# Layer 1's factors go through DRAM as rows, GpSimd weights and joins the sums, and one turn follows

## Chip, core and metric

The kernel runs on one core of a Trainium2 chip. All data are float32. The metric is the time of the device in microseconds (us), as the median of several runs. A profile of one execution shows where the time goes. The engines are named as in the profile: PE (TensorE, matmuls), PEld (its weight loads), DVE (VectorE), ACT (ScalarE), POOL (GpSimd) and SP, which issues most DMA transfers.

## The reference

Two layers of attention over a picture of 64 x 64 positions (N = 4096 tokens), with C = 256 channels and a batch of 2. Layer 0 has 4 heads of 16 channels, a normalization, and a factor per row (`dyn`). The change is in layer 1, which has 4 heads of 64 channels:

```
qkv = einsum('oc,bchw->bohw', w_qkv, x) + b_qkv
q, k, v = split(qkv.reshape(b, 4, 192, N), 3, axis=2)
attn = softmax(einsum('bhdn,bhdm->bhnm', q, k) / 8, axis=-1)
out = einsum('bhnm,bhdm->bhnd', attn, v).reshape(b, c, h, w)
return einsum('oc,bchw->bohw', w_out, out) + b_out + x
```

The product of `attn` and `v` is reshaped as it lies (tokens first, then channels) into the shape of the picture. So the kernel needs it with tokens on the partitions before it writes it away.

## The kernel before

Layer 0 is done in blocks of 512 tokens. Behind it, layer 1 goes over 32 units. A unit (b, g, j) is one batch, one pair of heads (g, heads k = 0 and 1) and one block of 512 queries. It has 32 chunks (m) of 128 keys. One pass of the last loop, a step, handles two chunks, so a unit has `US` = 16 steps. The program keeps an order written out by hand: `seq` holds every compute instruction at its place on its engine, and `at(t, place, ...)` hangs an extra piece of work on step t, at the place "start", "early", "early end", "late", "late end" or "end". DMA transfers are issued by SP in the order in which a scheduler places them, and SP waits at each one for what it needs.

For a chunk, PE computes the scores of both heads into PSUM (`score`, L885). DVE folds them into a running maximum (`keep`, L902), and ACT copies them to SBUF (L903). Eleven steps later (`LAG`) DVE adds the negative maximum (`shift`, L960), ACT takes the exponential (`weigh`, L972), POOL adds the weights to a running sum (L982 for the first two chunks, L984 for the others), and PE multiplies with the values (`gather`, L1013). The chunks wait in a ring of 26 buffers (`raw`); a buffer is filled again when POOL and PE have used it.

The maximum is taken in two groups n of 16 chunks. After each group, PE turns the maxima (`turn_max`, L915), DVE reduces them (`fold`, L932), SP writes them to DRAM (`neg`) and reads them back as a row for all partitions (`row`), and ACT places them in PSUM (`place_shift`, L952). The two groups of a unit thus have sums and products of different maxima: `lose` (L945) takes the difference, and `keep_total`, `add_sums` and `factors` make from it and the sums the two factors per query and head, f, in the form of tokens on partitions (POOL L1126, L1127, L1134, DVE L1133). Then `turn_sums` has PE turn each group's product (L1060, into the bank `misc`), `rows` has DVE multiply it with its factor out of PSUM (L1144), and POOL adds the value bias (L1150) and joins the two (L1153). SP writes the result to `att` (L1158).

PSUM has one bank named `misc`. The turns share it with the projections that are made for later units: for the first 24 units keys and values of the next pair of heads (`next_keys`, `next_values`, quarter by quarter, and the ACT copies `k1s` and `v1s`), for the last 8 units the outputs of batch 0 (`project_out`, the ACT copy `y`, and POOL's add L1181). With t1 = t0 + 24 for a unit that starts at step t0, the sums are at t1 + 4 to 8, and the two turns at t1 + 9. A pool `xb` with three buffers holds blocks of x that are fetched for keys, values and queries, in the passage between the layers too (values v0 to v7 of the first unit). The last unit has a path of its own (`last_rows`, `late_sums`), and after it PE finishes batch 1's outputs from `att` (L1295).

Of the kernel before, what the change touches and what calls it, by code (L numbers as in the profile page):

```python
# [8 lines left out]
F32 = mybir.dt.float32  # L9
AF = mybir.ActivationFunctionType  # L10
ALU = mybir.AluOpType
# [3 lines left out]
P = 128  # L15
NB = 512
# [4 lines left out]
D1 = 64  # L21
# [5 lines left out]
def conv_attention_kernel(  # L27
# [19 lines left out]
    nc = tc.nc  # L47
    B, _, N = x.shape
    NJ = N // NB
    NM = N // P  # L50
    PB = NB // P

    const = ctx.enter_context(tc.tile_pool(name="const", bufs=1))
    dram = ctx.enter_context(tc.tile_pool(name="dram", bufs=1, space=bass.MemoryType.DRAM))
# [157 lines left out]
    def at(t, place, step):  # L212
        extras.setdefault((t, place), []).append(step)
# [19 lines left out]
    with own0:  # L233
# [417 lines left out]
        def misc(name):  # L651
            return small_bank[0](name)

        def fetch(key, src, tag="xb", bufs=3, pool=l1x):
            t = pool.tile([P, CC, NB], F32, tag=tag, bufs=bufs, name=f"{tag}_{key}")
            nc.sync.dma_start(out=t, in_=src.rearrange("(c p) n -> p c n", p=P))
            loaded[key] = t
# [110 lines left out]
    with (  # L768
# [6 lines left out]
    ):  # L775
        small_bank[0] = lambda name: psm.tile([P, NB], F32, tag="misc", name=name)
        rmax, negs, rows_in, shifts, raws, accs = {}, {}, {}, {}, {}, {}
        avs1, srows, losts, joined, halves = {}, {}, {}, {}, {}
        rts = [None, None]
        outs = {}  # L780
        halves_of = {}
# [12 lines left out]
        }  # L794
        sum1 = {
            u: dram.tile([NG * 2, NB], F32, tag="sum_{}_{}_{}".format(*u), name=f"sum_{u}")
            for u in units
        }
        first, begun, late = {}, set(), {}
# [120 lines left out]
        def fold(u, n, k):  # L920


            b, g, j = u
            if k == 0:
                negs[u, n] = small.tile(
                    [P, 2, PB], F32, tag="negs", bufs=2 * NG, name=f"negs_{b}_{g}_{j}_{n}"
                )
                rows_in[u, n] = l1.tile(
                    [P, 2, NB], F32, tag="row", bufs=1, name=f"row_{b}_{g}_{j}_{n}"
                )  # L930
            nm, to = negs[u, n][:, k, :], neg1[u, n][k : k + 1, :]
            seq(nc.vector.tensor_reduce(  # L932
                nm, rts[k].rearrange("p (i m) -> p i m", m=P), AX.X, ALU.max, negate=True
            ))
            nc.sync.dma_start(
                out=to.rearrange("o (a p i) -> p (o a) i", p=P, i=2),
                in_=nm.rearrange("p (a i) -> p a i", i=2),
            )
            nc.sync.dma_start(out=rows_in[u, n][:, k, :], in_=to.partition_broadcast(P))

        def lose(u):

# [62 lines left out]
        def gather(t):  # L1005
            u = b, g, j = units[t // NM]
            m = t % NM
            n = m // GS
            if m % GS == 0:
                avs1[u, n] = psv.tile([P, NB], F32, tag="av", name=f"av1_{b}_{g}_{j}_{n}")  # L1010
            v = vs[b, g, m // PB]
            for k in range(2):
                seq(nc.tensor.matmul(  # L1013
                    avs1[u, n][k * D1 : (k + 1) * D1, :], v[:, m % PB, k, :], raws[t][:, k, :],
                    start=(m % GS == 0), stop=(m % GS == GS - 1),
                ))
            if on_tensor(t) and t % 2 == 1 and t != 2 * END - 1:
                late_sums((t - 1, t) if on_tensor(t - 1) else (None, t))
            elif t == 2 * END - 2:
                late_sums((t, t + 1))  # L1020
            raws.pop(t - 2, None)
            if m % GS == GS - 1:
                a = l1.tile([P, NB], F32, tag="avs", name=f"avs1_{b}_{g}_{j}_{n}")
                seq(nc.scalar.copy(a, avs1.pop((u, n))))
                avs1[u, n] = a

# [30 lines left out]
        def turned(a, name):  # L1057
            ps = misc(name)
            for i in range(PB):
                seq(nc.tensor.transpose(ps[:, bass.ts(i, P)], a[:, bass.ts(i, P)], ident))  # L1060
            return ps.rearrange("p (i k d) -> p k i d", k=2, d=D1)
# [67 lines left out]
        def factors(u):  # L1129

            b, g, j = u
            f = small.tile([P, NG, 2, PB], F32, tag="f1", name=f"f1_{b}_{g}_{j}")
            seq(nc.vector.reciprocal(f[:, 1], srows.pop(u)[:, 1]))  # L1133
            seq(nc.gpsimd.tensor_tensor(f[:, 0], f[:, 1], losts.pop(u), ALU.mult))  # L1134
            joined[u] = f

        def turn_sums(u, n):
            avs1[u, n] = turned(avs1[u, n], "turned_{}_{}_{}_{}".format(*u, n))

        def rows(u, n):  # L1140
            b, g, j = u
            ps = avs1.pop((u, n))
            r = l1.tile([P, 2, PB, D1], F32, tag="rows", name=f"rows_{b}_{g}_{j}_{n}")
            seq(nc.vector.tensor_tensor(  # L1144
                r, ps, joined[u][:, n].unsqueeze(3).to_broadcast([P, 2, PB, D1]), ALU.mult
            ))
            if n == 1:
                halves[u] = r
                bias = b1v[:, 2 * g : 2 * g + 2, :].unsqueeze(2).to_broadcast([P, 2, PB, D1])
                seq(nc.gpsimd.tensor_tensor(r, r, bias, ALU.add))  # L1150
                return
            joined.pop(u)
            seq(nc.gpsimd.tensor_tensor(r, r, halves.pop(u), ALU.add))  # L1153


            to = att[b].rearrange("(h q) (s d) -> h (q s) d", h=H, d=D1)
            for k in range(2):
                nc.sync.dma_start(  # L1158
                    out=to[2 * g + k, bass.ts(j, NB), :].rearrange("(i q) d -> q i d", q=P),
                    in_=r[:, k, :, :],  # L1160
                )
# [37 lines left out]
        for n, u in enumerate(units):  # L1199
# [29 lines left out]
            if u != units[-1]:  # L1229
                at(t1 + 4, "late", lambda u=u: total(u))  # L1230
                at(t1 + 5, "start", lambda u=u: keep_total(u))
                at(t1 + 1, "late", lambda u=u: lose(u))
                at(t1 + 7, "late end", lambda u=u: add_sums(u))
                at(t1 + 8, "end", lambda u=u: factors(u))
                for place, k in (("early", 1), ("late", 0)):
                    at(t1 + 9, place, lambda u=u, k=k: turn_sums(u, k))
                    at(t1 + 9, f"{place} end", lambda u=u, k=k: rows(u, k))
            else:
                at(END + 1, "late", lambda u=u: last_lost(u))
                at(END + 4, "early", lambda u=u: late_sums((None, None)))  # L1240
                at(END + 4, "early end", lambda u=u: keep_late(0))
                at(END + 5, "early", lambda u=u: turn_late(0))
                at(END + 5, "early end", lambda u=u: add_late(u, 0))
                at(END + 6, "early", lambda u=u: turn_sums(u, 0))
                at(END + 6, "early end", lambda u=u: first_rows(u))
                at(END + LAG, "late", lambda u=u: turn_late(1))
                at(END + LAG, "late", lambda u=u: add_late(u, 1))
                at(END + LAG, "late", lambda u=u: turn_sums(u, 1))
                at(END + LAG, "late", lambda u=u: last_rows(u))
# [17 lines left out]
        def fetch_last(i, pool, tag, bufs=1):  # L1267

            t = pool.tile([P, CC, NB], F32, tag=tag, bufs=bufs, name=f"x_last_{i}")
            nc.sync.dma_start(out=t, in_=x1[B - 1][i].rearrange("(c p) n -> p c n", p=P))  # L1270
            last_x[i] = t
# [7 lines left out]
        def fetch_second_half(i):  # L1279

            t = ring.tile([P, 2, NB], F32, tag="raw", name=f"att_last_{i}")
            for k in range(2):
                r, n = k * D1, D1 - NB // D1
                nc.sync.dma_start(
                    out=t[r : r + n, :, :].rearrange("p i n -> p (i n)"),
                    in_=att[B - 1][P + r : P + r + n, bass.ts(i, 2 * NB)],
                )
            last_att[i] = t
# [31 lines left out]
            last_half(j, c, ps)  # L1320
            add_half(j, ps, c == 0)

        for i in range(3):
            at(END - 11 + 2 * i, "start", lambda i=i: fetch_last(i, l1x, "xb", 3))
        at(END - 5, "start", lambda: fetch_last(3, l1, "xo"))
        at(END - 3, "start", lambda: fetch_last(4, l1, "ao"))
        at(END - 10, "start", lambda: fetch_first_half(2, l1x, "q", 2))
        for i in range(2):
            at(END - 2, "start", lambda i=i: fetch_first_half(i, l1, "kv", 2))
        for i in range(NJ // 2):  # L1330
            at(END + 3 + i // 2, "start", lambda i=i: fetch_second_half(i))
        for i in range(EARLY, NJ):
            at(END + 5, "start", lambda i=i: fetch_first_half(i, l1o, f"k{i}"))
        for i in range(5, NJ):
            at(END + 5 + (i - 5) // 2, "start", lambda i=i: fetch_last(i, ring, "raw", None))
        FILL = {(END, "early end"): 0, (END + 1, "early"): 1, (END + 2, "early"): 2}
        for (t, place), j in FILL.items():
            at(t, place, lambda j=j: whole_half(j, 0))
# [93 lines left out]
```

## Time and profile before

| | |
|---|---|
| median of 3 runs | 4652.29 us (4652.22 to 4654.23) |
| profiled execution | 4653.08 us, span 4651.2 us |
| granted TensorE clock | 0.997 of full speed |
| PE busy | 4461.5 us, 96% |
| DVE busy | 3894.5 us, 84% |
| ACT busy | 3439.9 us, 74% |
| POOL busy | 2515.1 us, 54% |
| layer 1, from the first score to the last unit's last turn | about 2058 to 4623 us |

The shares are means over two layers: in layer 0 POOL does almost nothing, and in layer 1 it is busy nine tenths of the time. So the profile is read by stages. A line of a group gives the source line, the engine, the operation, output and input by their names with their shapes, the count, and then the busy time, the mean duration in ns, and the idle time of the engine before it with what ended it. A line of the waits gives who waited for whom, with the sum in us, the number of times and the longest. A line of the order in time begins with its start from the span's start and its duration, both in us. Busy PE is modelled and not PE at its peak.

### The profile page before, as it was taken

The numbers are of one execution on the slowest core, as the hardware profiler recorded it, in microseconds if no ns is written. First come the engines' busy times: TensorE is split into PE (matmuls) and PEld (weight loads), VectorE is DVE, ScalarE is ACT, GpSimd is POOL, SyncE is SP. The second block draws the span as 40 slices with busy tenths as digits, with TensorE's granted clock in tenths as the row PEclk, the third lists the DMA queues.
The fourth block names the chain that finished last, engine by engine and source line by source line (L and its number), as shares of the span: only waits on it lengthen the run. The fifth ranks groups of instructions, "written<-read, shape, count | busy, mean of one in ns | idle before, by whom it ended". The sixth has DMA issues, their size and how long they took to land. (4 is left out here: it accounts for less than half of the span.)

```text
span 4651.2 us, 72702 instructions
## 1 busy us (share of the span) xinstructions
PE 4461.5 (96%) x28242; PEld 1497.3 (32%) x28242; DVE 3894.5 (84%) x4506; ACT 3439.9 (74%) x4588; POOL 2515.1 (54%) x1306
## 2 busy tenths in 40 slices
PE   8999999999999999999999999999999999999998
PEld 3433333333333333332333333333333333222222
DVE  6777777777777777539999999999999999999997
ACT  3366666666666666668888888888888888888885
POOL 5300000000000000008999999999999999999995
PEclk9999999999999999999999999999999999999999
DMA  3100000000000000121111221111211112121213
GB/s 100 39 4 20 20 20 15 15 15 15 15 15 15 15 14 14 35 71 41 33 42 35 62 50 37 37 39 42 71 42 37 37 35 62 48 53 37 53 39 111
DMA packets 199689, 174.81 MB, mean 38 GB/s; under 512 B 121256, under 2 KB 122088, under 8 KB 199344
## 3 DMA queue, kind: packets, MB, share of 16 engines
q1 hardware_dynamic: 197488, 169.58, 14.6%
q8 instruction: 221, 3.62, 0.3%
q14 instruction: 124, 1.02, 0.1%
q10 hardware_dynamic: 1856, 0.59, 0.1%
HBM read 127.65 MB, written 42.48 MB: 37 GB/s over the span
## 5 line engine op out<-in xcount | busy, mean ns | idle before, releaser
L984 POOL TENSOR_TENSOR acc<-acc,raw 128x1024 f32<-128x1024 f32 x883 | 2096.0, 2374 | 72.0 <-ACT raw L972 15.1
L402 DVE TENSOR_REDUCE mx<-a 128x1 f32<-128x512 f32 x2048 | 1315.3, 686 | 449.0 <-PE a L398 448.0
L439 ACT ACTIVATE p<-s 128x512 f32<-128x512 f32 x2048 | 1107.9, 595 | 702.1 <-PE a L398 369.4
L885 PE MATMUL s<-q,k 64*128 64x512 f32 x4096 | 1130.4, 637 | 127.6 <-ACT raw L903 121.0
L960 DVE TENSOR_TENSOR raw<-raw,shift 128x1024 f32<-128x1024 f32 x1024 | 1236.8, 1212 | 7.1 <-ACT shift L952 6.2
L436 PE MATMUL s<-q,kT 32*128 32x512 f32 x4096 | 1217.8, 640 | 0.0
L902 DVE TENSOR_TENSOR rmax<-s,rmax 128x1024 f32<-128x1024 f32 x960 | 1169.5, 1218 | 48.3 <-PE s L885 37.3
L972 ACT ACTIVATE raw<-raw 128x1024 f32<-128x1024 f32 x1024 | 1086.1, 1061 | 144.6 <-DVE raw L960 109.2
L903 ACT COPY raw<-s 128x1024 f32<-128x1024 f32 x1024 | 1035.7, 1011 | 166.5 <-DVE rmax L902 105.5
L398 PE MATMUL a<-kT,q 32*128 32x512 f32 x4096 | 1129.2, 643 | 1.4 <-DVE mx L402 1.3
L1013 PE MATMUL av<-raw,v 128*64 128x512 f32 x4096 | 1014.2, 608 | 10.0 <-ACT raw L972 6.5
L451 PE MATMUL av<-p,v 128*32 128x256 f32 (+1 forms) x7904 | 650.1, 399 | 0.6 <-ACT avs L465 0.6
L501 POOL TENSOR_TENSOR f<-f,dyn 128x16 f32<-128x16 f32 x15 | 3.3, 221 | 1027.4 <-DVE f L500 1027.4
L885 PEld LDWEIGHTS s<-q,k 64*128 64x128 f32 x4096 | 316.8, 185 | 704.1 <-ACT raw L903 541.9
L436 PEld LDWEIGHTS s<-q,kT 32*128 32x128 f32 x4096 | 397.0, 183 | 425.9 <-issue 392.8
L1013 PEld LDWEIGHTS av<-raw,v 128*64 128x64 f32 x4096 | 239.7, 135 | 666.5 <-issue 444.6
L451 PEld LDWEIGHTS av<-p,v 128*32 128x32 f32 x7904 | 157.7, 108 | 751.4 <-issue 737.2
L552 POOL TENSOR_SCALAR res<-res 128x1024 f32<-128x1024 f32 x16 | 16.7, 1044 | 659.1 <-ACT res L551 659.1
L398 PEld LDWEIGHTS a<-kT,q 32*128 32x128 f32 x4096 | 305.1, 183 | 31.5 <-DVE mx L402 18.2
L982 POOL TENSOR_TENSOR acc<-raw,raw 128x1024 f32<-128x1024 f32 x64 | 152.7, 2386 | 118.7 <-ACT raw L972 74.8
L932 DVE TENSOR_REDUCE negs<-rt 128x4 f32<-128x512 f32 x126 | 87.0, 690 | 58.5 <-PE rt L915 58.5
L915 PE MATMUL rt<-ident,rmax 128*128 128x128 f32 x504 | 82.7, 287 | 9.3 <-ACT v1s L841 5.7
(335 smaller groups left out, 1767.1 us busy)
## 6 DMA issues: line engine op xcount, KB each, us to landing
row<-neg SPq DMA_DIRECT2D x128, 256.0 KB
x<-in_x_dram SPq DMA_DIRECT2D x16, 512.0 KB
res<-in_x_dram SPq DMA_DIRECT2D x16, 512.0 KB
x<-res SPq DMA_DIRECT2D x16, 512.0 KB
att<-rows SPq DMA_DIRECT2D x62, 128.0 KB
kd<-k1s SPq DMA_DIRECT2D x24, 256.0 KB
vd<-v1s SPq DMA_DIRECT2D x24, 256.0 KB
k<-kd SPq DMA_DIRECT2D x24, 256.0 KB
```

Source lines behind the costliest of these rows:

```text
L398: seq(nc.tensor.matmul(ps, qs0[u][r, bass.ts(i, P)], kTs[b][r, bass.ts(m, NB)], start=True, stop=True,))
L402: seq(nc.vector.tensor_reduce(mxs[u][:, i * H + h, m : m + 1], ps, AX.X, ALU.max))
L436: seq(nc.tensor.matmul(ps, kTs[b][r, bass.ts(m, P)], qs0[u][r, :], start=True, stop=True))
L439: seq(nc.scalar.activation(pt[:, k, :], ps, AF.Exp, scale=D0**-0.5))
L451: seq(nc.tensor.matmul(avs[u][32 * h : 32 * h + 32, cols], vs0[b][:, m, 32 * h : 32 * h + 32], pts[t, h // 2][:, h % 2, cols], start=(m == ...
L885: seq(nc.tensor.matmul(ps[:, k, :], ks[b, g, m // PB][r, bass.ts(m % PB, P)], qs1[u][r, :], start=True, stop=True,))
L902: seq(nc.vector.tensor_tensor(rmax[u, n], ps, before, ALU.max))
L903: seq(nc.scalar.copy(raw, ps))
L960: seq(nc.vector.tensor_tensor(raws[t], raws[t], shifts[u, t % NM // GS], ALU.add))
L972: seq(nc.scalar.activation(p, p, AF.Exp, scale=D1**-0.5))
L984: seq(nc.gpsimd.tensor_tensor(accs[u, n], accs[u, n], p, ALU.add))
L1013: seq(nc.tensor.matmul(avs1[u, n][k * D1 : (k + 1) * D1, :], v[:, m % PB, k, :], raws[t][:, k, :], start=(m % GS == 0), stop=(m % GS == GS ...
```

## The change

The factors f are written to a new DRAM buffer `fac` and read back as rows: `facs`, 512 queries along a row, each head's row repeated over the 64 partitions of its channels. This is the form in which the products lie before they are turned. POOL multiplies each group's product with its row (`weight`, at t1 + 11), adds the two and adds the bias as a value per partition (`join`, at t1 + 12). One turn follows at t1 + 14 (`turn_rows`), and ACT copies it from PSUM to SBUF (`rows`). The two DVE multiplications are gone.

The maxima of both heads are read back with one transfer of 1024 numbers per partition, after the second head's have been written. `xb` has two buffers instead of three, `avs` three instead of two. Near the end, fetches of x for the last outputs move to other buffers and steps, and `att`'s second half is read four steps later.

```diff
-        def fetch(key, src, tag="xb", bufs=3, pool=l1x):
+        def fetch(key, src, tag="xb", bufs=2, pool=l1x):
...
+        fac1 = {
+            u: dram.tile([NG * 2, NB], F32, tag="fac_{}_{}_{}".format(*u), name=f"fac_{u}")
+            for u in units
+        }
...
-            nc.sync.dma_start(out=rows_in[u, n][:, k, :], in_=to.partition_broadcast(P))
+            if k == 1:
+                nc.sync.dma_start(
+                    out=rows_in[u, n].rearrange("p k n -> p (k n)"),
+                    in_=neg1[u, n].rearrange("k n -> (k n)").partition_broadcast(P),
+                )
...
-                a = l1.tile([P, NB], F32, tag="avs", name=f"avs1_{b}_{g}_{j}_{n}")
+                a = l1.tile([P, NB], F32, tag="avs", bufs=3, name=f"avs1_{b}_{g}_{j}_{n}")
...
-            joined[u] = f
+            nc.sync.dma_start(
+                out=fac1[u].rearrange("m (a p i) -> p (m a) i", p=P, i=2),
+                in_=f.rearrange("p n k (a i) -> p (n k a) i", i=2),
+            )
+            joined[u] = []
+            for n in range(NG):
+
+                pool, tag = (l1o, f"k{2 + 5 * n}") if u == units[-2] else (l1, "kv")
+                row = pool.tile([P, NB], F32, tag=tag, name=f"facs_{b}_{g}_{j}_{n}")
+                for k in range(2):
+                    m = 2 * n + k
+                    nc.sync.dma_start(
+                        out=row[k * D1 : (k + 1) * D1, :],
+                        in_=fac1[u][m : m + 1, :].partition_broadcast(D1),
+                    )
+                joined[u].append(row)
+
+        def weight(u, n):
+
+            a = avs1[u, n].rearrange("p (a i m) -> p a i m", m=P, i=2)
+            f = joined[u][n].rearrange("p (a m i) -> p a i m", m=P, i=2)
+            seq(nc.gpsimd.tensor_tensor(a, a, f, ALU.mult))
+
+        def join(u):
+
+            joined.pop(u)
+            a = avs1.pop((u, 0))
+            seq(nc.gpsimd.tensor_tensor(a, a, avs1.pop((u, 1)), ALU.add))
+            seq(nc.gpsimd.tensor_scalar(a, a, b1[:, u[1], 2:3], None, ALU.add))
+            avs1[u] = a
+
+        def turn_rows(u):
+            avs1[u] = turned(avs1[u], "turned_{}_{}_{}".format(*u))
...
-        def rows(u, n):
+        def rows(u):
             b, g, j = u
...
-            seq(nc.vector.tensor_tensor(
-                r, ps, joined[u][:, n].unsqueeze(3).to_broadcast([P, 2, PB, D1]), ALU.mult
-            ))
...
+            r = l1.tile([P, 2, PB, D1], F32, tag="rows", name=f"rows_{b}_{g}_{j}")
+            seq(nc.scalar.copy(r, avs1.pop(u)))
...
-                for place, k in (("early", 1), ("late", 0)):
-                    at(t1 + 9, place, lambda u=u, k=k: turn_sums(u, k))
-                    at(t1 + 9, f"{place} end", lambda u=u, k=k: rows(u, k))
+                for k in range(NG):
+                    at(t1 + 11, ("early end", "late end")[k], lambda u=u, k=k: weight(u, k))
+                at(t1 + 12, "early end", lambda u=u: join(u))
+                at(t1 + 14, "early", lambda u=u: turn_rows(u))
+                at(t1 + 14, "early end", lambda u=u: rows(u))
...
-        for i in range(3):
-            at(END - 11 + 2 * i, "start", lambda i=i: fetch_last(i, l1x, "xb", 3))
-        at(END - 5, "start", lambda: fetch_last(3, l1, "xo"))
-        at(END - 3, "start", lambda: fetch_last(4, l1, "ao"))
+        for i in range(2):
+            at(END - 5 + 3 * i, "start", lambda i=i: fetch_last(i, l1x, "xb", 2))
+        at(END - 4, "start", lambda: fetch_last(2, l1, "xo"))
+        at(END - 3, "start", lambda: fetch_last(3, l1, "ao"))
...
-            at(END + 3 + i // 2, "start", lambda i=i: fetch_second_half(i))
+            at(END + 7 + i // 2, "start", lambda i=i: fetch_second_half(i))
...
-        for i in range(5, NJ):
-            at(END + 5 + (i - 5) // 2, "start", lambda i=i: fetch_last(i, ring, "raw", None))
+        for i in range(4, NJ):
+            at(END + 5 + (i - 4) // 2, "start", lambda i=i: fetch_last(i, ring, "raw", None))
```

More of the change, by code (lines that the diff above doesn't have):

```diff
@@ L777, in conv_attention_kernel @@
         rmax, negs, rows_in, shifts, raws, accs = {}, {}, {}, {}, {}, {}
-        avs1, srows, losts, joined, halves = {}, {}, {}, {}, {}
+        avs1, srows, losts, joined = {}, {}, {}, {}
         rts = [None, None]
@@ L1137, in turn_sums @@
         def turn_sums(u, n):
             avs1[u, n] = turned(avs1[u, n], "turned_{}_{}_{}_{}".format(*u, n))
-        def rows(u, n):
+        def rows(u):
             b, g, j = u
-            ps = avs1.pop((u, n))
-            r = l1.tile([P, 2, PB, D1], F32, tag="rows", name=f"rows_{b}_{g}_{j}_{n}")
-            seq(nc.vector.tensor_tensor(
-                r, ps, joined[u][:, n].unsqueeze(3).to_broadcast([P, 2, PB, D1]), ALU.mult
-            ))
[L1147 to L1153, printed above, removed]
+            r = l1.tile([P, 2, PB, D1], F32, tag="rows", name=f"rows_{b}_{g}_{j}")
+            seq(nc.scalar.copy(r, avs1.pop(u)))
```

## The prediction

> **What bounds the kernel now.** I read the groups of layer 1 first, then the waits of VectorE and of GpSimd within single units, then the order in time. The groups from 2150 us on (columns: busy us, mean ns, idle before and who ended it):
>
> ```profile
> L984 POOL TENSOR_TENSOR acc<-acc,raw 128x1024 f32<-128x1024 f32 x868 | 2060.4, 2374 | 69.5 <-ACT raw L972 13.7
> L960 DVE TENSOR_TENSOR raw<-raw,shift 128x1024 f32<-128x1024 f32 x1003 | 1211.5, 1212 | 5.0 <-ACT shift L952 4.1
> ...
> L1144 DVE TENSOR_TENSOR rows<-turned,f 128x512 f32<-128x512 f32 x62 | 42.4, 683 | 1.2 <-issue 1.2
> ...
> L1153 POOL TENSOR_TENSOR rows<-rows,rows 128x512 f32<-128x512 f32 x31 | 39.8, 1282 | 2.3
> L1150 POOL TENSOR_TENSOR rows<-rows,b1v 128x512 f32<-128x512 f32 x31 | 39.7, 1280 | 0.0
> ```
>
> The view of stretches shows four engines near their limit: of 2300 to 2600 us, PE is busy 283.1, DVE 287.0, ACT 265.8, POOL 280.3. So I take one unit (16 steps of two chunks). Its period is the distance between the first sums on POOL (L982): 2894.88 to 2974.03, 79.15 us. In the last eight units, which also make batch 0's outputs, it is 79.36 (4243.23 to 4322.59). POOL's waits in those two stretches, in this order:
>
> ```profile
> POOL acc L982 <- ACT raw L972: 2.7, 2, 2.0
> POOL acc L984 <- ACT raw L972: 0.2, 1, 0.2
> ```
> ```profile
> POOL acc L982 <- ACT raw L972: 0.7, 1, 0.7
> ```
>
> POOL has 2.9 us to spare in an early unit, 0.7 in a late one (two adds L1181 of 1.28 us took the rest). DVE has next to nothing: its operations start 1.13 us after each other. Where they don't, PE is late. This is the place where the changed kernel puts its turn (three engines, merged in time):
>
> ```profile
> 2943.74 0.67 ACT L820 ACTIVATE k1s<-k1p,b 128x512 f32<-128x512 f32 x1
> ...
> 2943.83 1.94 PE L1013 MATMUL av<-raw,v 128*64 128x512 f32 x8
> ...
> 2946.06 1.21 DVE L960 TENSOR_TENSOR raw<-raw,shift 128x1024 f32<-128x1024 f32 x1
> ...
> 2946.14 2.29 PE L885 MATMUL s<-q,k 64*128 64x512 f32 x8
> ...
> 2947.31 1.23 DVE L902 TENSOR_TENSOR rmax<-s,rmax 128x1024 f32<-128x1024 f32 x1
> ```
>
> The maximum starts 1.25 us after the shift, not 1.13: its score (1.1 us from 2946.14) has only just come. PE runs without a gap from 2943.83. So in steps with projection quarters PE and DVE bind together, and PE work put there costs its full length. A second place is where the rows are made now: there DVE alone binds, and PE waits for it.
>
> ```profile
> 2920.59 0.68 DVE L1144 TENSOR_TENSOR rows<-turned,f 128x512 f32<-128x512 f32 x1
> 2921.19 1.22 DVE L902 TENSOR_TENSOR rmax<-s,rmax 128x1024 f32<-128x1024 f32 x1
> ```
>
> **Pages.** The Trainium skill's "GPSIMD Engine Reference", section 7 (Performance pitfalls for Q7 kernels), says that reading SBUF with a step of more than 8 bytes costs half as much again per element. The factor rows are read in steps of two floats, exactly 8 bytes, so no surcharge. No POOL row of this trace has such a read; I take 1.28 us (L1153) and keep 1.9 as the upper end. "DMA: Bandwidth & Descriptors", section "Anatomy of one DMA", puts some 2 us of fixed cost on a transfer, mostly the write's receipt. The trace agrees: the write of the maxima was issued at 2914.80, the read that waits for it at 2917.74, 2.9 us with issue. The forecast goes by the trace.
>
> **The change part by part.**
>
> Rows off DVE. Two operations fewer per unit. From start to next start each took 0.60 (2920.59 to 2921.19), so 1.20 us. PE does not stand in the way there: without the two turns it waits for ACT's copies, which follow DVE. I follow the chain score, maximum, copy for the next six chunks and find 1.19 us kept. PE also loses one group of four transposes, and the wait for L1144 inside it (36.5 us in all): slack, worth nothing.
>
> One turn, moved five steps, into the place shown above. In the built order on PE it stands between the scores and the av products of the step in which ACT makes `k1s` (in the last eight units `y`, 670 ns, the same place). Turn and `k1p` share the one bank `misc`, so PE must wait for `k1s`, which ends at 2944.41; PE is free at 2943.83. The wait is 0.6 us. The transposes take 0.6 (the same form on L915 starts 0.59 before the av products behind it: 2953.33 to 2953.92). Queued behind it on PE: av, v1p, then the score that DVE takes next, 1.2 us late. v1p needs the bank again, after ACT's new copy of the rows: `exp` ends at 2946.27, the copy about 0.6 later (L1024's form, 599 ns), v1p would be due at 2946.83: 0.05 more. Sum 1.25 us that DVE waits. Net per early unit: +1.25 - 1.19 = +0.06. This happens in 22 early units: +1.3 us. ACT's 0.6 us itself is hidden by this wait; ACT idles 6 us per unit.
>
> POOL. Out: two operations (2 x 1.28). In: two weightings and a sum (3 x 1.28) and a bias add. For that, two rows are near: 767 ns at L315 (two operations with per-partition values, same shape) and 1044 at L552 (double length, constants); I take 0.70, ends 0.55 and 0.80. With 1.30 from start to start, +2.0 us per unit. In an early unit 2.9 us were idle: hidden, with 0.9 left; with no idle it would cost 2.0. In a late unit 0.7 was idle, so POOL needs 79.36 + 1.3 = 80.66 us, while DVE and PE need 79.42. POOL becomes the bound: +1.24 each. POOL may fall behind by the ring of 26 `raw` tiles: by times of copies and sums, a sum now ends 2 to 5 us before its tile is filled again, so the first 1.5 us are swallowed and the last unit's share partly falls in the tail, where POOL idles (4.83 us before 4588). Eight units: 8 x 1.24 - 1.5 - 1.2 = +7.2 us.
>
> The way through DRAM. Per unit SP issues five more transfers (one write, four reads of `facs`) and two fewer (one `row` read per group instead of two), 0.35 to 0.43 us each, beside a queue that mostly waits. The two `att` writes go out five steps later, behind `kd`; their readers come units later, but for the tail. In the built order on SP: both `neg`, `fac`, `row`, four `facs`. `fac` waits for POOL's f, and `row` stands behind it; the shift copy on ACT and then DVE wait for `row`. f is done at 2919.80; `row` would be issued near 2920.2, where its second half now goes at 2925.11. Better, worth nothing: ACT waits for `row` only 2.6 us in all. `facs` then lands: layer 0's same pair (L502 issued 361.4, product L512 begun 367.4) takes 6.0 us; with `row` ahead (512 KB; the packet records of the two reads issued from 2958.21 on run from 2959.5 to 2964.1, 4.6 us) 8 to 10 us. Between f and the first weighting POOL has five sums, 12.2 us. Hidden with 2 to 4 us left; each us beyond costs a late unit a us.
>
> One read for both heads. The first head's row goes later by the second fold, 2.4 us. The shift copy at 2967.38 came 7 us after the last issue of `row`: hidden. Without cover, up to 2.4 us on ACT.
>
> Two `xb` buffers, and the passage between layers. v6 was fetched at 2031.24; now it waits for v4's product, 2047.8, and PE wants it at 2049.4. A 512 KB fetch lands in 4 to 5 us (estimate: the one issued at 2906.62 has its last packet at 2909.8, and some 1.5 of completion), so PE waits 2 to 3, of which the wait for the last layer-0 product (2052.88) hides 2: +1 us (0 to 3).
>
> Tail. The last but one unit's rows leave the chain (DVE rows, 1.22 us of waiting, rows again, POOL rows: some 1.2 us gained), but its turn comes ahead of the last unit's, with a bank wait of 1 us, and its factors queue behind 2 MB of x loads: +0.5 (-2 to +4).
>
> Sum against the profiled execution (4653.08; span 4651.2): 1.3 + 7.2 + 1 + 0.5 = +10. The median of the runs shown is 4652.29, so 4662.3. What measures as a change here is about 0.2%, 9.3 us.
>
> **Rivals.**
>
> Faster: the turn is hidden. If PE finds the bank free and the turn delays the next score by d < 0.4 us, DVE keeps its 1.2. Then an early unit is set by POOL: 79.15 - 2.9 + 2.0 = 78.2, a gain of 0.9 x 22 = 20; the late eight still lose 7, passage and tail 1.5: 4640 to 4642. It decides at d = 0.4 (22 x 0.8 less 8.5 is 0.2%). For it: DVE's start-to-start of 1.13 nearly everywhere, 36 us of rows. Against: the 1.25 above, and the same bank wait that stops PE at L915 after v1s (22.6 us, 21 times).
>
> Much slower: the factors come late. If `facs` lands 5 us later than reckoned (queue full of k and v loads), POOL stalls some 2 us; early units have 0.9 left, so 1.1 x 22 + 2 x 8 = 40 more: 4700. For it: layer 0's product waited for its factors 59.4 us in 9 of 15 cases. Against: 12.2 us of sums in between.
>
> POOL's new reads cost more (1.9 us each): +1.2 per unit; early 0.3 x 22, late 1.2 x 8: 4678.
>
> The change not being made as said: the built order shows every operation where the text puts it; 1 in 100.
>
> **Numbers.** My forecast 0.60, with own range 4654 to 4673, half above 4661.6; turn hidden 0.17; late factors 0.10; dear POOL reads 0.12; rest 0.01. Faster 0.18, same 0.29, slower 0.53. Leaving out a tenth at each end, the range goes from 4638 to 4690.
>
> **What would show it.** Right: early unit period near 79.2, a new DVE wait for PE of some 1.2 us per unit behind the turn, the turn waiting for ACT k1s; late period near 80.6, ACT copies waiting for POOL acc, no POOL idle; bias add near 0.7 us. Wrong: an early period of 78 (turn hidden), POOL waiting for `facs`, or late units still at 79.4 (POOL's work cheaper than reckoned).

## The result, and the profile after

The changed kernel took 4694.83 us (median of 4 runs, 4694.21 to 4697.62), the kernel before 4652.39: a ratio of 1.0091 (95% interval 1.0078 to 1.0104). That is slower, as forecast, but by 42 us instead of 10, and above the range of 4638 to 4690. Later runs fell on other chips. There the kernel before took 4648 each time, and the changed one, run again, 4678.66: a ratio of 1.0065 (1.0051 to 1.0078). So the second loss is smaller than the first by more than a quarter. That turned out to be a clue. One execution among the experiments below (of `two_reads`: 5934.84 us at a granted clock of 0.654, where its others had 0.985 to 0.987) is a slow one and is left out of its ratio, though not of its median.

Where the time went, by stretches of the profiled executions. The start of a unit is its first maximum on DVE. "Early" and "late" are the medians over one unit; the sums add up to the span.

| us | before | after |
|---|---|---|
| up to the first unit's start | 2062.55 | 2061.95 |
| first unit | 60.1 | 59.6 |
| next 23 units, sum (early unit) | 1822.8 (79.16) | 1844.3 (80.17) |
| next 7 units, sum (late unit) | 555.7 (79.36) | 570.9 (81.52) |
| last unit and tail | 150.1 | 155.7 |
| span | 4651.2 | 4692.4 |

Three stretches carry the loss: 21.5 us in early units, 15.2 in late ones, 5.6 in the tail. The passage between the layers costs nothing.

The groups of layer 1 in the profile after, from 2150 us on (busy us, mean ns, then idle before and who ended it; the second block is the shift copy's line in the kernel before):

```profile
L992 POOL TENSOR_TENSOR acc<-acc,raw 128x1024 f32<-128x1024 f32 x867 | 2057.8, 2373 | 92.8 <-ACT raw L980 37.3 <-POOL acc L990 0.2 <-POOL acc L992 0.2
L968 DVE TENSOR_TENSOR raw<-raw,shift 128x1024 f32<-128x1024 f32 x1002 | 1210.5, 1212 | 37.9 <-ACT shift L960 37.8
...
L1164 POOL TENSOR_TENSOR avs<-avs,facs 128x512 f32<-128x512 f32 x62 | 79.2, 1301 | 5.5 <-DMA facs<-fac_(1, 1, 6)_19414 5.5
L960 ACT COPY shift<-row 128x1024 f32<-128x1024 f32 x62 | 68.8, 1109 | 43.2 <-DMA row<-neg 38.7 <-DVE rmax L906 2.6
L1171 POOL TENSOR_SCALAR avs<-avs,b 128x512 f32<-128x512 f32 x31 | 48.5, 1563 | 3.1
L1170 POOL TENSOR_TENSOR avs<-avs,avs 128x512 f32<-128x512 f32 x31 | 39.7, 1280 | 0.0
```
```profile
L952 ACT COPY shift<-row 128x1024 f32<-128x1024 f32 x62 | 69.1, 1114 | 6.4 <-DMA row<-neg 3.1
```

Two rows are not as forecast. The bias add (L1171) takes 1563 ns, not 0.70 us. And DVE's shift (L968) now waits 37.8 us for ACT's shift copy (4.1 before), which itself waits 38.7 us for the row of the maxima (3.1 before). In one early unit this wait stands here (ACT, then DVE; start and duration in us):

```profile
2936.94 1.11 ACT L960 COPY shift<-row 128x1024 f32<-128x1024 f32 x1 [1.17 <-DMA row<-neg]
...
2938.09 1.22 DVE L968 TENSOR_TENSOR raw<-raw,shift 128x1024 f32<-128x1024 f32 x1 [1.03 <-ACT shift L960]
```

The transfers ahead of it, from SP's order in time. The fold's two writes (`neg`) go out, then the factors of the unit before (`fac`), and only then the read (`row`):

```profile
2923.12 2.81 SPq L939 DMA_DIRECT2D neg<-negs  x2
2928.15 0.36 SPq L1143 DMA_DIRECT2D fac_(0, 1, 1)_19393<-f  x1
2928.62 0.52 SPq L944 DMA_DIRECT2D row<-neg  x1
2933.02 2.37 SPq L1154 DMA_DIRECT2D facs<-fac_(0, 1, 1)_19393  x4
```

The packet records of this queue run in the order of issue: `fac`'s 1024 packets of 8 bytes from 2929.04 to 2929.71, `row`'s 128 packets of 4096 bytes from 2931.44 to 2936.12, then `facs`. For the 28 rows of middle units that have `fac` ahead of them, the first packet comes 2.68 us after the issue and the last is done after 6.91 (medians). For the 28 rows of the first halves, which have no `fac` ahead, it is 0.97 and 3.98.

The turn, in the same way, at its new place (ACT, PE, DVE):

```profile
2951.99 0.67 ACT L824 ACTIVATE k1s<-k1p,b 128x512 f32<-128x512 f32 x1
...
2952.80 0.63 PE L1068 MATMUL turned<-ident,avs 128*128 128x128 f32 x4 [0.66 <-ACT k1s L824]
...
2954.30 1.21 DVE L968 TENSOR_TENSOR raw<-raw,shift 128x1024 f32<-128x1024 f32 x1
2956.84 1.23 DVE L906 TENSOR_TENSOR rmax<-s,rmax 128x1024 f32<-128x1024 f32 x1 [1.33 <-PE s L889]
```

The next maximum starts 2.54 us after the shift, where it was 1.25 before: 1.29 us, by a bank wait of 0.66 and transposes of 0.63. In the late units the transposes wait in the same way for `y`, and in neither kind of unit for GpSimd's bias add. From the waits of 2300 to 4500 us:

```profile
PE turned L1068 <- ACT k1s L824: 13.8, 21, 0.7
PE turned L1068 <- ACT y L1205: 4.6, 7, 0.7
```

### The profile page after: what moved, and what is told of

Read it like the earlier page. It is cut to its first block, busy times and chain, and to the rows that moved or that the text cites. A ratio compares the mean times of both kernels' runs of the same rounds, so it can differ in the third digit from the quotient of the medians.

```text
span 4692.4 us, 72638 instructions
## 1 busy us (share of the span) xinstructions
PE 4446.3 (95%) x28118; PEld 1485.0 (32%) x28118; DVE 3861.0 (82%) x4444; ACT 3449.4 (74%) x4619; POOL 2599.6 (55%) x1368
## 4 chain that ended last, share of the span: by engine, by line
PE 62%; DVE 11%; POOL 8%; issue 7%; DMA 7%; ACT 5%; SPq 0%; POOLq 0%; ACTq 0%; DVEq 0%
PE s L436 24%; PE av L451 12%; DVE rmax L906 8%; PE av L1021 8%; PE s L889 7%; POOL acc L992 6%; DMA row<-neg 4%; ACT raw L907 3%; DVE raw L968 3%; PE a L398 2%; DMA neg<-negs 2%; PE rt L919 1%; PE p L258 1%; ACT raw L980 1%; PE o L537 1%
## 5 line engine op out<-in xcount | busy, mean ns | idle before, releaser
L968 DVE TENSOR_TENSOR raw<-raw,shift 128x1024 f32<-128x1024 f32 x1024 | 1237.1, 1212 | 38.2 <-ACT shift L960 38.1
L960 ACT COPY shift<-row 128x1024 f32<-128x1024 f32 x64 | 71.0, 1109 | 43.2 <-DMA row<-neg 38.7
```

What stands on the lines that cost most here:

```text
L968: seq(nc.vector.tensor_tensor(raws[t], raws[t], shifts[u, t % NM // GS], ALU.add))
```

## The experiments

Theory A: the row of a second half is late because it stands behind `fac`. Theory B: the joint read is late by itself. Theory C: GpSimd's load, through the bias add, is the loss. Theory D: the turn at its place is. All ratios are to the kernel before on the same chip. The last three columns come from the one profiled execution of each kernel, which can lie off its median: by -3.8 us for `no_bias`, +2.7 for `turn_later`, +2.2 for `row_first_no_bias`, +2.1 for `two_reads`, and by 1.0 or less for the others.

| kernel | us | ratio (95%) | early | late | last unit, tail |
|---|---|---|---|---|---|
| changed, again | 4678.66 | 1.0065 (1.0051 to 1.0078) | 79.59 | 80.92 | 155.4 |
| `row_first` | 4667.81 | 1.0043 (1.0029 to 1.0057) | 79.24 | 81.36 | 155.3 |
| `no_bias` | 4664.44 | 1.0034 (1.0022 to 1.0047) | 79.48 | 79.61 | 151.2 |
| `no_bias_again` | 4664.85 | 1.0037 (1.0024 to 1.0049) | 79.78 | 79.86 | 150.7 |
| `turn_later` | 4677.26 | 1.0062 (1.0049 to 1.0074) | 79.53 | 81.12 | 155.5 |
| `two_reads` | 4799.31 | 1.0323 (1.0309 to 1.0337) | 84.33 | 84.59 | 157.2 |
| `row_first_no_bias` | 4654.91 | 1.0017 (1.0010 to 1.0024) | 79.24 | 79.42 | 156.5 |
| `row_first_tail` | 4664.17 | 1.0036 (1.0024 to 1.0049) | 79.24 | 81.37 | 152.5 |
| `row_first_turn1` | 4664.94 | 1.0037 (1.0024 to 1.0051) | 79.04 | 81.35 | 156.7 |
| `all4` | 4645.40 | 0.9995 (0.9987 to 1.0003) | 78.61 | 79.72 | 150.3 |
| `four_act` | 4628.36 | 0.9958 (0.9944 to 0.9971) | 77.95 | 79.76 | 153.6 |
| `before_joint` | 4647.40 | 0.9999 (0.9991 to 1.0007) | 79.16 | 79.34 | 149.5 |

**The row ahead of the factors** (`row_first`). Both transfers are held in program order, in which the row comes first:

```diff
-                nc.sync.dma_start(
+                seq(nc.sync.dma_start(
                     out=rows_in[u, n].rearrange("p k n -> p (k n)"),
...
-            nc.sync.dma_start(
+            seq(nc.sync.dma_start(
                 out=fac1[u].rearrange("m (a p i) -> p (m a) i", p=P, i=2),
```

> Edit: on the SP queue the read of the maxima (`row`) of a unit's second half is kept ahead of the previous unit's factors (`fac`); in the changed kernel it stands behind them in 31 units. Nothing else moves. Theory A (the row is late because it stands behind `fac`, whose 1024 packets of 8 bytes go first and which itself waits for GpSimd): the row's packets start about 1.1 us after its issue instead of 2.8, the shift copy of the second half starts 10.2 us after the fold instead of 11.3 to 12.8, its wait for the row goes, early units fall from 80.2 to about 79.2, late ones by 0.7 to 1.3 until GpSimd is the bound: 22 x 1.0 + 8 x 1.0 = 30 us less, about 4665. Theory B (one read of both heads must wait for the second head's write, and is late whoever stands before it): the copy still starts at 11 us or later, 4690 to 4697. Theory C (GpSimd's load alone): early units unchanged, 4690.

SP's order in the same unit:

```profile
2913.42 2.81 SPq L939 DMA_DIRECT2D neg<-negs  x2
2918.93 0.34 SPq L944 DMA_DIRECT2D row<-neg  x1
2919.32 0.43 SPq L1143 DMA_DIRECT2D fac_(0, 1, 1)_19393<-f  x1
```

Over 56 rows the first packet now comes 0.96 us after the issue, the last is done after 3.77, and the shift copy of the second half starts 10.28 us after the second fold, with hardly a wait:

```profile
L960 ACT COPY shift<-row 128x1024 f32<-128x1024 f32 x62 | 69.4, 1119 | 5.7 <-DMA row<-neg 2.0
```

Early units take 79.24 us, one like the other. Theory A holds for them, and B and C fall there. The time was 4667.81 against an expected 4665; how much of that is a gain depends on the chip: 22 us by the first ratio (1.0091 to 1.0043), 10 by the second (1.0065 to 1.0043), where the two intervals just overlap. Late units hardly fell: 81.36, their seven together 567.2 us against 570.9 and, in the second profile, 568.6. There theory A's part of the expectation failed. GpSimd waits for nothing in such a unit, and the transposes and ACT's copies now wait for it (waits of 2300 to 4500 us):

```profile
ACT raw L907 <- POOL acc L992: 12.3, 23, 1.0
...
PE turned L1068 <- POOL avs L1171: 7.5, 6, 1.3
```

**The bias add left out** (`no_bias`).

```diff
-            seq(nc.gpsimd.tensor_scalar(a, a, b1[:, u[1], 2:3], None, ALU.add))
```

> Edit: GpSimd's bias add is left out in the 31 units that are turned as rows, so their values lack the bias; all else is the changed kernel. Theory C (GpSimd's 1.56 us bias add is on the path everywhere): 31 x 1.56 = 48 us less, about 4646. Theory A (early units are bound by the late row, GpSimd has slack there; late units by GpSimd, which also makes the factors and so the row late): early units stay at 80.2, the 8 late ones fall by 1.2 to 2.0, and the tail by up to 1.5: 11 to 17 us less, 4678 to 4684.

Late units fell to 79.61 as theory A had it. But early units were shorter than 80.2 as well, and the time fell between the two theories: 14 us under A's range, 18 over C's figure. Early units were shorter with the turn moved, too (below). I could not tell the effect from that of the chip, and so ran the changed kernel again beside it:

> The changed kernel itself, beside the kernel without the bias add on the same chip. Open: leaving the bias add out shortened the early units by 0.7 us, which no theory foresaw, and moving the turn to t1 + 17 by 0.6; in both, the rows that stand behind `fac` had their last packet 6.4 us after issue (median), in the first profile of the changed kernel 6.9. Theory A (that is the chip's or the execution's DMA speed): here the changed kernel too shows 6.3 to 6.5 and early units of 79.4 to 79.7, 4675 to 4684 where the kernel before takes 4648. Theory C (GpSimd's bias add itself lengthens early units): 6.9 or not, early units stay at 80.0 to 80.3, 4688 to 4692.

> GpSimd's bias add left out (31 units lack the bias), a second time, beside the changed kernel. Theory A: early units as the changed kernel has them on this chip, within 0.2 us; late units near 79.6; 12 to 16 us under it. Theory C: early units 0.6 to 0.8 us under it; 24 to 28 us under it.

It was the chip (or the moment; the runs don't part the two), not the bias add: that is theory A's expectation. In the changed kernel run again the rows behind `fac` were done after 6.55 us instead of 6.91, its early units took 79.59, and the kernel without the bias add was 13.8 us under it, with early units no shorter (79.78). This fits the clue from the result: the row comes in later than the moment at which it is needed, so tenths of a microsecond of transfer time are passed on to every early unit. The waits of the shift copy in the early units add up to 23.9 us in the first profile of the changed kernel and to 11.6 in the second, and those units differ by 13.7. The kernel before, whose row may come 1.26 us later, varies by 0.1%.

With the row first, the bias add can be measured by itself (`row_first_no_bias`, both edits):

> Edits: the row kept ahead of the factors, and GpSimd's bias add left out (the values of 31 units lack the bias). Base: the kernel with the row first alone, whose early units take 79.24 us, late ones 80.2 to 82.5, its tail 155.3. Theory (the loss has separate terms: the row's place in early units, GpSimd's bias add in late units and the tail, the turn in all): early units stay at 79.24, since GpSimd has slack there; GpSimd's work in a late unit falls from 80.0 to 78.4, under the others, so late units fall to 79.3 to 79.6, which is 6 x 1.9 = 11 us, and the tail by 3 to 4: about 4653, 0.1% above the kernel before. Rival (GpSimd loses time in late units to its waits for exponentials and factors rather than to the bias add): late units stay at 80.5 or more, 4660 to 4668.

Early units stayed at 79.24, late ones fell from 81.36 to 79.42, 11.3 us over the seven. The theory's figures hold for the units. The tail did not fall in this profile (156.5, expected 151 to 152), and the time is 2 us over the expectation; as the profiled execution is itself 2.2 us over the median, how long the tail usually is stays open.

**The turn three steps later** (`turn_later`).

```diff
-                at(t1 + 14, "early", lambda u=u: turn_rows(u))
-                at(t1 + 14, "early end", lambda u=u: rows(u))
+                turn = t1 + (14 if u == units[-2] else 17)
+                at(turn, "early", lambda u=u: turn_rows(u))
+                at(turn, "early end", lambda u=u: rows(u))
```

> Edit: the turn and the copy of its rows move from step t1 + 14 to t1 + 17 (not for the last turned unit), where the bank has been free for a step. Theory D (the turn behind `k1s` costs 1.25 us of VectorE in each unit, beside the late row): early units fall by 1.2, late ones by 1.2 plus up to 1.5 of the turn's wait for the bias add: 22 x 1.2 + 8 x 2 = 42 us less at most, about 4653 to 4668. Rival (the path's loss is all in the late row, or the turn costs the same wherever it is put, by its own transposes and the bank): no more than 10 us less, 4685 to 4697.

The time, 4677.26, lies between the two ranges. Against the changed kernel run again (4678.66, another chip on which the kernel before also took 4648) it is no gain: theory D's did not come. The turn did not wait for `k1s` any more, but the next user of the bank, `v1p`, did not find it free: it waits for ACT's copy of the turned rows, and the first half's shift copy starts at 11.42 us instead of 10.21.

```profile
PEld v1p L836 <- ACT rows L1183: 47.0, 21, 2.2
PE v1p L836 <- ACT rows L1183: 28.5, 21, 1.4
```

**Two reads again** (`two_reads`): the transfer of the kernel before put back into the changed one.

```diff
-            if k == 1:
-                nc.sync.dma_start(
-                    out=rows_in[u, n].rearrange("p k n -> p (k n)"),
-                    in_=neg1[u, n].rearrange("k n -> (k n)").partition_broadcast(P),
-                )
+            nc.sync.dma_start(out=rows_in[u, n][:, k, :], in_=to.partition_broadcast(P))
```

> Edit: the maxima come back by one read for each head, as in the kernel before; all else is the changed kernel. Theory B (the joint read is what makes the row late): the first head's row leaves 0.5 us after its fold again, the shift copy starts at 10.2 us, early units at 79.2, about 4665 to 4670. Theory A (it is the place behind `fac`): the second head's read still stands behind `fac` and an extra read shares the queue, the copy starts no earlier than 11.3 us, 4692 to 4705.

Theory B is refuted, but the loss is far outside A's range too: some 120 us over the changed kernel run again. (The granted clock was 0.985 instead of 0.996; what part of the loss goes with that is not separated.) SP's order shows where the row waits:

```profile
2963.36 0.36 SPq L939 DMA_DIRECT2D neg<-negs  x1
2966.44 0.34 SPq L943 DMA_DIRECT2D row<-neg  x1
2966.83 0.43 SPq L939 DMA_DIRECT2D neg<-negs  x1
2968.39 0.36 SPq L1139 DMA_DIRECT2D fac_(0, 1, 1)_19393<-f  x1
2975.49 0.34 SPq L943 DMA_DIRECT2D row<-neg  x1
```

The second head's write is issued behind the first head's read. Its packets run from 2969.02, when that read is nearly done, together with `fac`'s, and the second read, which must wait for that write, goes out 8.7 us after it (in the kernel before, in the unit of the prediction, 7.0). The shift copy starts 13.1 us after the fold (2978.86, after a wait of 2.86). So the joint read is the part of the change that limits the damage of the new order. By itself, in the kernel before (`before_joint`), it should be neutral:

> Edit to the kernel before: both heads' maxima come back by one read, nothing else of the change. Theory (the joint read is hidden in itself, for the shift copy of the second half starts at 11.47 us behind VectorE's two row operations, and without `fac` ahead of it the row is there by 10.2): within 0.1% of the kernel before, units 79.15 to 79.4, first full unit 78 to 79. Rival (the joint read is late by itself, as it waits for the later head's write): units longer by 0.3 to 1.1, +10 to +30 us. Second rival (two reads were costing the kernel before something): units 78.5 to 79.0, 5 to 15 us less.

It is: 0.9999. The shift copy of the second half still starts at 11.47 us, held by DVE's two row operations. Only the second unit, in which no rows are made yet, is shorter: 77.89 against 79.14.

**The end** (`row_first_tail`). In the changed kernel the last row and the last factors stand behind fetches of `x_last`, and GpSimd waits for the factors:

```profile
4618.60 0.97 SPq L939 DMA_DIRECT2D neg<-negs  x2
4620.63 3.13 SPq L1302 DMA_DIRECT2D x_last<-x  x2
4625.53 0.33 SPq L944 DMA_DIRECT2D row<-neg  x1
4625.95 0.39 SPq L1143 DMA_DIRECT2D fac_(1, 1, 6)_19414<-f  x1
4633.24 2.59 SPq L1154 DMA_DIRECT2D facs<-fac_(1, 1, 6)_19414  x4
...
4637.53 2.55 POOL L1164 TENSOR_TENSOR avs<-avs,facs 128x512 f32<-128x512 f32 x2 [5.48 <-DMA facs<-fac_(1, 1, 6)_19414]
```

```diff
+                    if u == units[-2]:
+                        seq(load)
...
+            if i >= 4:
+                seq(load)
```

(`load` is the read of `facs` in the first place and the fetch of `x_last` in the second.)

> Edits: the row kept ahead of the factors, and on SP at the end the last factors' reads kept ahead of the fetches of `x_last` 4 to 7, which stand before the last row in the changed kernel. Theory (the tail's 5 us come from the last row and the last factors standing behind these fetches, so that GpSimd waits 5.5 us for the factors): the last row is issued about 3 us earlier against its fold, the 5.5 us wait falls to under 2, the stretch after the last unit's start falls from 155.3 to 151 to 153: 4664 to 4665. Rival (the tail is longer by GpSimd's weights and bias add): 155 as before, 4668; or the late x_last now holds the projections: 157, 4670.

The last unit and tail went from 155.3 to 152.5, the time to 4664.17, both as expected, though the row goes only 1.9 us earlier against its writes, not 3; the wait for the factors (4.91 with the row first) is 0.36. The remaining 2.4 us over the kernel before are not explained by a run. One candidate is untested: GpSimd's first sum of the last unit starts 64.1 us after the unit's first maximum, and 60.0 in the kernel before, so it enters the tail 4 us further behind.

**The turn one step after a fold** (`row_first_turn1`), 25 instead of 17 in the edit above, and t1 + 14 for the last two turned units.

> Edits: the row kept ahead of the factors, and the turn with its row copy moved from t1 + 14 to t1 + 25 (one step after a fold, the place in which the kernel before turned; the last two turned units keep t1 + 14), so that it waits neither for `k1s` nor for the bias add. Theory (of the turn's 1.25 us, 0.6 is the wait for `k1s` to free the bank and 0.6 the transposes, and in late units it waits up to 2 us for the bias add): early units fall from 79.24 to 78.6, late ones to 80.0 to 80.5 where GpSimd's own work is the bound: 22 x 0.6 + 6 x 1.2 = 20 us less, about 4648. Rival (a turn costs VectorE 1.25 wherever it stands, as moving it three steps showed): 79.2 and 81, 4662 to 4668.

Early units only fell to 79.04, and neither story is right. The wait for the bank is gone, but ACT's copies now wait for GpSimd:

```profile
ACT raw L907 <- POOL acc L992: 87.7, 159, 1.4
```

GpSimd waits 1.3 us in all in 2300 to 3900 us. So 79.04 is GpSimd's own work in an early unit, and 81.36 (2 x 1.28 more, less a little) in a late one, the figure in every kernel that has the bias add and the row first. In most late units the turn has moved away from the bias add here and they are no shorter, so it was not the turn's wait that set them in `row_first`. In this kernel the turn no longer sets the time. To see its price, GpSimd had to be relieved:

> Edits together: the row first, the turn at t1 + 25, the last factors' reads ahead of x_last, and the bias moved to the values before they are stored (sum of weights over sum of weights is 1, so a bias on each value comes out once): GpSimd adds it to `v1s` once in each of the early units (about 1.28 us), the bias adds on the sums go, 31 on GpSimd and 2 on VectorE at the end. Theory: GpSimd needs 77.0 in early units and 78.4 in late ones, so early units take 78.6, late ones 78.8 to 79.4, the tail 150 to 152: 4648 + 8 - 22 x 0.6 - 3 = 4632 to 4642, faster than the kernel before by 0.1 to 0.3%. Rival (the turn costs 1.25 anywhere): 79.2 in all units, 4648 to 4655, no gain on the kernel before.

`all4` moves the bias to the values (a GpSimd add of 1289 ns on `v1s`, and on the first values in the passage). It was even with the kernel before, over the expected range. Early units came as expected (78.61) and follow GpSimd's work, which waits 0.9 us in all from 2300 to 3900 us. But late units took 79.72, 0.3 over their range, and the passage grew by 7.4 us (first unit's start at 2069.98), which I had not counted. ScalarE took the bias better (`four_act`):

```diff
-            seq(nc.gpsimd.tensor_scalar(a, a, b1[:, u[1], 2:3], None, ALU.add))
             avs1[u] = a
+
+        def bias(u):
+            a = avs1[u]
+            seq(nc.scalar.activation(a, a, AF.Identity, bias=b1[:, u[1], 2:3]))
...
+                at(t1 + (13 if u in units[-3:-1] else 22), "early end", lambda u=u: bias(u))
```

> Edits to the changed kernel: the row first, the turn at t1 + 25 (t1 + 14 for the last two turned units), the last factors' reads ahead of x_last, and the bias added on ScalarE (one in-place copy with a per-partition bias) at t1 + 22, between the join and the turn, in place of GpSimd's. Theory (GpSimd is the bound once the row and the turn are out of the way: 79.03 in early units and 81.37 in late ones with the 1.56 us bias add, so 77.5 and 79.8 without it; ScalarE is busy 70 of 80 us and has room for 0.6): early units 78.0 to 78.5, late ones 79.4 to 79.9, the start of the first unit as in the kernel before, the tail 150 to 152: 4648 - 22 x 0.9 + 7 x 0.4 + 1 = 4632, range 4626 to 4642, faster than the kernel before by 0.1 to 0.5%. Rival (ScalarE's order is as tight as VectorE's, and 0.6 us more on it costs a unit 0.6 to 1.2): early units 78.6 to 79.2, 4642 to 4655.

```profile
L1177 ACT ACTIVATE avs<-avs,b 128x512 f32<-128x512 f32 x31 | 21.9, 707 | 2.1 <-POOL avs L1172 2.1
```

4628.36 us, 0.42% under the kernel before (0.9944 to 0.9971), within the expected range. Early units take 77.95, a little under theirs, and the tail 153.6, over the 150 to 152 expected. The changed kernel's second unit, in which nothing is turned yet, takes 77.90; measured by that unit, the turn and the bias together cost 0.05 us at this place. Late units (79.76) follow GpSimd's work once more: it waits for nothing from 4000 to 4480 us. So the change as an idea gains, once its order on SP, the engine of its bias add and the turn's place are other ones. `four_act` changes them together with the tail's order; what each gives beside the others was not measured, and the turn's place gave nothing as long as GpSimd set the time.

## Why the prediction was wrong, point by point

By the spans the forecast missed by 31 us: 20 in the early units (21.5 against 1.3), 8 in the late ones (15.2 against 7.2, of which it put a part in the tail), 5 in the tail (5.6 against 0.5), less 2 in the passage and the first unit (-1.1 against +1).

**"Better, worth nothing: ACT waits for `row` only 2.6 us in all."** This step failed, and it made the forecast's early units too short by 1 us each in the first profile (0.4 in the second). The order on SP (`fac`, then `row`) was read rightly, and so was the time of the issue. Two things were not drawn from it. First, the row's deadline moved. In the kernel before, the second half's shift copy starts 11.47 us after the fold, for DVE's row operations hold it there, and that hid a late row; without them it is due at 10.21. The 1.19 us "kept" were kept only if the row came 1.2 us earlier. Second, I compared times of issue (2920.2 with 2925.11) and not of arrival. In the kernel before SP's order is this:

```profile
2914.80 0.36 SPq L935 DMA_DIRECT2D neg<-negs  x1
2917.74 0.34 SPq L939 DMA_DIRECT2D row<-neg  x1
2918.13 0.43 SPq L935 DMA_DIRECT2D neg<-negs  x1
2925.11 0.34 SPq L939 DMA_DIRECT2D row<-neg  x1
```

Over the second halves of 27 middle units (medians), the last row is issued 6.82 us after the fold in the kernel before and 3.40 in the changed one. But its last packet is done after 10.91 and after 10.50 (9.88 in the second profile): of 3.4 us gained at issue 0.4 to 1.0 are left at arrival, less than the 1.26 by which the deadline moved. With the row first it is 7.06.

On one queue `fac`'s small packets go first. The Trainium skill's "DMA: Bandwidth & Descriptors", section "Queues, rings and completion order", says that each DMA engine takes its descriptors in ring order, and the packet records agree. The price is 2.68 us to the row's first packet instead of 0.97; why 1.7 us pass between `fac`'s last packet and the row's first (2929.71 and 2931.44) is not shown. Together with the turn, which takes what DVE gained, early units lost 0.4 to 0.9 us by it, 9 to 23 us in all, depending on the chip or the moment.

The profile of before did show it, in one place. In the second unit no rows are made yet, and there the second half's shift copy sat idle for 1.31 us and started at 11.46 us all the same, so that the unit took 79.14. (The view puts this wait down to DVE's maximum, which ended at that moment, 2136.61; but the row's last packet is done at 2136.21.) With the joint read alone (`before_joint`) the wait is gone and the unit takes 77.89.

**"Bias add ... I take 0.70, ends 0.55 and 0.80."** Mis-sized: 1563 ns, nearly twice the upper end. The near row that I took (767 ns at L315, two operations on the same shape) is the speed that "GPSIMD Engine Reference", section 3.1, measured for 512 elements in its best loop (769 ns), and this one-operation form with a value per partition does not reach it. Why is not shown. It is not the company of a busy VectorE: the adds take 1557 to 1566 ns whether VectorE works beside them all the time or for 0.95 us, and L315 takes 767 to 770 with 0 to 0.85 us of it. GpSimd's need in a late unit is thus 81.36 and not 80.66, and leaving the add out gives back 11.3 us of the seven late units.

**Late units: "POOL becomes the bound: +1.24 each".** Right in mechanism. With the row first GpSimd is the bound (81.36, and 81.35 with the turn moved away), 0.7 over the figure, which is nearly the bias add's 0.86. "The first 1.5 us are swallowed" was too little: with the row first, GpSimd's first sum of a unit starts 59.4 us after the unit's first maximum in the early units, 61.8 and 63.8 in the first two late ones, and 63.0 to 64.2 in the others. It falls 4.7 us behind, and while it does so the units take 79.42 and 80.97.

**"In an early unit 2.9 us were idle: hidden, with 0.9 left".** Hidden, but with 0.2 left: 79.04 against 79.24.

**The turn, "1.25 us".** Right: 1.29, in the parts that were named. With the row first, the early unit is 79.24 against 79.16 before, +0.08, where I had +0.06.

**Weights and the eight-byte step.** Right: 1301 ns against 1280 for L1170, no surcharge, as "GPSIMD Engine Reference", section 7, has it. Dear reads fall as a rival.

**Factors through DRAM.** Hidden in all units but the last (5.5 us of waiting in all). The rival "factors come late" gave 4700, near the result, but it is not what happened: it was the factors' write that made another transfer late.

**One read for both heads.** Hidden, as said (`before_joint`); that the changed kernel loses far more without it (`two_reads`) was not seen.

**Passage and tail.** The passage was put at +1 and cost nothing (-0.6). The tail was put at +0.5, up to +4, and took 5.6: the queue behind the x loads was named, but not that the last `row` stands in it too.

## What to carry to other kernels

When work is taken off an engine, look at what came in late behind it unnoticed: its deadline moves forward by what was removed, and a wait near zero in the old profile says nothing about the new one. A small write put ahead of a read on the same queue was paid for by the reader here, so look at packets' times and not at those of issue, and keep the order by hand where a scheduler would go by readiness. Price an operation by the row of its exact form, and where there is none, take a range that has twice the nearest row in it.

## What the runs showed of the hardware

- A GpSimd add of one value per partition to 128x512 floats takes 1563 ns, against 1280 for the sum of two such tensors, 767 for L315's two-operation form, and 707 ns for the same bias on ScalarE.
- A read of 512 KB issued 0.7 us (median) behind a write of 1024 packets of 8 bytes has its first packet 1.7 us later than without it (2.68 us after its issue against 0.97), though these packets themselves are on record for 0.67 us only.
- The same program, 0.1% apart on different chips before, was 0.3% apart after (4694.83 and 4678.66). Its row's arrival then differed by 0.6 us (10.50 and 9.88 after the fold) and was part of its path; that this is the reason is a reading, as chip and moment were not parted.
